# Layer-0 experts of a two-layer ViT tower: tokens sorted by expert through DRAM into 60 blocks

## The chip, the cores and the metric

The kernel runs on one core of a Trainium2 chip. A core has a matrix engine (TensorE, PE in the profile, with PEld for the loading of its weights), a vector engine (DVE), a scalar engine (ACT), a general one (POOL) and SyncE (SP), each with an instruction queue of its own that is worked off in order; SP, ACT and POOL can issue DMA transfers, which run on 16 shared DMA engines. The metric is the device time of the core in microseconds, the median of the runs of one kernel.

## The reference

Everything is float32. Four images of 3 x 224 x 224 become 784 patch tokens of 256 features each, which the tokenizer concatenates three times. Two layers follow: attention and a mixture of experts in each. The part that matters here is the mixture of layer 0, on 4 x 784 = 3136 distinct tokens:

```python
def _L0_ffn_ref(features, ...):                      # features: layer norm of h
    E, D, H, TOP_K = (6, 256, 256, 2)
    rh = jax.nn.relu(features @ router_w1 + router_b1)             # 128 wide
    expert_logits = jax.nn.softmax(rh @ router_w2 + router_b2, axis=-1)
    top_w, top_i = jax.lax.top_k(expert_logits, TOP_K)
    routing_weights = jax.nn.softmax(top_w, axis=-1)
    h1 = jax.nn.relu(jnp.einsum('bsd,edh->bseh', features, expert_w1) + expert_b1)
    h2 = jax.nn.relu(jnp.einsum('bseh,ehf->bsef', h1, expert_w2) + expert_b2)
    expert_out = jnp.einsum('bsef,efo->bseo', h2, expert_w3) + expert_b3
    sel = jnp.take_along_axis(expert_out, top_i[:, :, :, None], axis=2)
    return jnp.sum(sel * routing_weights[..., None], axis=2)
...
h = h + _L0_attn_ref(_layernorm(h, axis=-1), ...)
h = h + _L0_ffn_ref(_layernorm(h, axis=-1), ...)
h = h + _L1_attn_ref(_layernorm(h, axis=-1), ...)
h = h + _L1_ffn_ref(_layernorm(h, axis=-1), ...)
```

As written, all six experts run on every token, and two of the six results are kept.

## The kernel before

It carries one of the three copies of the tokens: 28 tiles of 112 tokens, 7 per image. The residual stream `h` stays in the on-chip memory, tokens on partitions: `h[TT, NT, D]` with TT = 112, NT = 28, D = 256. Stages follow each other: tokenizer, attention of layer 0, experts of layer 0, linear attention of layer 1, experts of layer 1, which also stores the result. A framework assigns buffers from pools, puts in the semaphore waits and orders the instructions of each engine's queue by priority; a pool that is closed gives its space to the next one opened, and the first use of that space waits for the last use of the old.

Products of a float32 operand take two records per instruction in the profile. A product reads its stationary operand into TensorE (PEld) and streams the columns of the other past it, into a bank of PSUM; there are seven such banks in the pool `psum` and one in `psum_s`. From there ACT or DVE must copy it out: `copy_out` (L71 on ACT, L73 on DVE) takes the two in turn, `bias_relu` (L78 on ACT, L80 on DVE) takes ACT two times in three. `transposed` (L227) turns tokens on partitions to features on partitions, by a product with an identity.

The experts of layer 0 (from the line `nxt = layer_input(work, 0, GT, "xT0")` on) go over 7 groups of 4 tiles (448 tokens). Per group: a router product (through `mm_t`, L236) with its relu (L504), the logits (L510), `top2` (L435 to L466: some 24 small vector instructions and two exponentials), which gives a weight for each of the six experts, 0 for those not chosen. Then the layer norm and the transposes of the next group, so that they lie between the experts' products. Then for each of the six experts two layers with features on partitions, two halves of 128 features each:

```python
pm = mm_t(GN, ew[e, i], slice(o * P, (o + 1) * P), lambda c: src[:, c, :], "pe")
bias_relu(dst[:, o, :], pm, col(b, 2 * e + o))
```

and the third with tokens on partitions (`mm_rows`, L247), whose result `add_weighted` (L487, DVE) multiplies with the expert's weight and adds to `h`. At the end of a group the weights are transposed (`weights_t`, L473, L475) and multiplied with the third bias (L537), which is added to `h` (L539). No transfer takes part in this stage but two weight loads for the next one (`Wqkv`, `Wout`) at its start. After it, the pool `lin` of layer 1's attention opens.

Of the kernel before, what the change touches and what calls it, by code (L numbers as in the profile page):

```python
"""ViT tower: patch tokenizer, one gated-attention + top-2 MoE layer, one linear-attention + top-2
gated-expert layer.

The tokenizer concatenates its tokens with themselves (q = k = tokens, so the sequence is three
copies of the 784 patch tokens).  Everything after it treats positions alike: rows are mapped
independently, and the two sums over the sequence (the attention logits of layer 0, the key norm and
key-value product of layer 1) are three times the sum over one copy, whatever the inputs.  The kernel
therefore carries one copy, puts the factor REP into those sums, and stores the rows three times.

Token tiles have 112 rows (7 per image).  The residual stream h stays in SBUF, tokens on partitions;  # L10
operands of the matrix products are transposed on the tensor engine to features on partitions.
"""
# [15 lines left out]
TT = 112  # tokens in a tile  # L28
NI = 4  # images
TPI = 7  # tiles in an image  # L30
# [10 lines left out]
GT = 4  # tiles in a group  # L41
# [3 lines left out]
E1 = 4  # L45
HEADS = 8
# [4 lines left out]
def tile_vit_tower(ctx: ExitStack, tc: tile.TileContext, a: dict, out: bass.AP):  # L51
# [15 lines left out]
    def copy_out(dst, src):  # L67
        """PSUM to SBUF, on the scalar and the vector engine in turn."""
        turn[0] += 1
        if turn[0] % 2:  # L70
            nc.scalar.copy(dst, src)  # L71
        else:
            nc.vector.tensor_copy(dst, src)  # L73
# [22 lines left out]
    rank = {}  # E, E-1, ..., 1 along the experts: the lower index wins a tie  # L96
# [5 lines left out]
    # Vectors that lie along partitions: rows of one tile, transposed once.  # L102
# [36 lines left out]
    def spread(pool, key, src):  # L139
        """A vector along the free dim, on all the partitions of a token tile."""  # L140
        n = src.shape[0]
        t = pool.tile([TT, n], F32, tag=key, name=key)
        nc.gpsimd.dma_start(out=t, in_=src.partition_broadcast(TT))
        return t

    def weight(pool, key, src, p=P, eng=nc.sync):
        """[K, N] as [p, K / p, N]."""
        k, n = src.shape
        t = pool.tile([p, k // p, n], F32, tag=key, name=key)
        eng.dma_start(out=t, in_=src.rearrange("(c p) n -> p c n", p=p))  # L150
        return t

# [1 line left out]
    # Partition (image, patch row); a strided view of the free dims is one patch column's patches.  # L154
# [28 lines left out]
    ew = {}  # L183
    for e in range(E0):
        for i, name in enumerate(("expert_w1", "expert_w2", "expert_w3")):
            ew[e, i] = weight(wts, f"ew{e}_{i}", a[f"L0_ffn_{name}"][e])
    eb3 = wts.tile([E0, D], F32, tag="eb3", name="eb3")
    nc.gpsimd.dma_start(out=eb3, in_=a["L0_ffn_expert_b3"])

    h = res.tile([TT, NT, D], F32, tag="h", name="h")  # L190

# [1 line left out]
    def ln_stats(src, n, twice=False):  # L193
        """Mean and 1 / sqrt(var + eps) of n tiles of rows.  twice: of a second layer norm, without
        an affine part between, as well: its input has mean 0 and variance var / (var + eps)."""
# [26 lines left out]
    def transposed(xn, n, put):  # L222
        """put(c, psum): the features c * 128... of n token tiles, on partitions."""
# [8 lines left out]
    def mm_t(n, w, wcols, xT, name, chunks=2):  # L232
        """(x @ w[:, wcols])^T, with the n columns of xT(c)."""
# [8 lines left out]
    def mm_rows(tiles, xT, w, name, chunks=2):  # L242
        """x @ w of up to two token tiles, in one PSUM bank: [TT, len(tiles), 256]."""
# [20 lines left out]
    with tc.tile_pool(name="tokw", bufs=2) as work:  # L264
        # Patches, features on partitions, tokens in the order of the sequence.
        pT = tokp.tile([KP, 2, NI * HP, HP], F32, tag="pT", name="pT")
        for w0 in range(0, HP, GT):
# [4 lines left out]
            for j in range(GT):  # L272
                # The reference has a patch's features in the order (y, x, channel).
# [57 lines left out]
    # Logits are dot products of whole images, per head: with (head, channel) on partitions,  # L331
    # products summed along the tokens, and then over a head's channels by a 0/1 matrix that leaves
    # the sum on each of them.
    scale = REP / math.sqrt(CHEAD) / math.sqrt(REP * SEQ)
    with tc.tile_pool(name="att", bufs=1) as attp:
# [3 lines left out]
        for tiles in groups:  # L339
# [3 lines left out]
            # The output bias goes into the residual now that the layer norm has read it.  # L343
# [77 lines left out]
    def top2(lg, n, E):  # L421
        """Routing weights over all experts, 0 off the two largest softmax(lg): softmax of those
        two probabilities.  lg: [TT, n, E], overwritten.  One more column of ones comes behind."""
# [35 lines left out]
        sel = chosen[0]  # L459
        nc.vector.tensor_tensor(sel, sel, chosen[1], ALU.add)  # L460
# [6 lines left out]
        return w  # L467

    def weights_t(pool, w, n, E):
        """w's tiles transposed: experts on partitions."""  # L470
# [21 lines left out]
    w1p = ctx.enter_context(tc.tile_pool(name="w1p", bufs=1))  # L492
    with tc.tile_pool(name="ffn0", bufs=2) as work:
# [3 lines left out]
        bout = spread(w1p, "bout", a["L1_attn_b_out"])  # L497

        nxt = layer_input(work, 0, GT, "xT0")
        for tiles in groups:  # L500
            t0 = tiles[0]
            xT = nxt
            rT = work.tile([P, GN], F32, tag="rT", name="rT")
            nc.scalar.activation(  # L504
                rT, mm_t(GN, rw1, slice(0, P), lambda c: xT[:, c, :], "pr"), AF.Relu,
                bias=col("router_b1"),
            )
            pr = psum_s.tile([P, 512], F32, tag="pss", name="plg")
            for j in range(GT):
                nc.tensor.matmul(  # L510
                    pr[:TT, j * E0 : (j + 1) * E0], rT[:, cut(j, 1)], rw2, start=True, stop=True
                )
            lg = small.tile([TT, GT, E0], F32, tag="lg0", name="lg0")
            nc.vector.tensor_tensor(
                lg, pr[:TT, : GT * E0].rearrange("p (j e) -> p j e", e=E0), over(rb2, GT), ALU.add
            )
            w = top2(lg, GT, E0)
            if t0 + GT < NT:
                nxt = layer_input(work, t0 + GT, GT, "xT0")
            for e in range(E0):  # L520
                src = xT
                for i, b in ((0, "eb1_0"), (1, "eb2_0")):
                    dst = work.tile([P, 2, GN], F32, tag=f"hid{i}", name=f"hid{i}")
                    for o in range(2):
                        pm = mm_t(
                            GN, ew[e, i], slice(o * P, (o + 1) * P), lambda c: src[:, c, :], "pe"
                        )
                        bias_relu(dst[:, o, :], pm, col(b, 2 * e + o))
                    src = dst
                for two in halves(range(GT)):  # L530
                    pm = mm_rows(two, lambda c, j: src[:, c, cut(j, 1)], ew[e, 2], "pe3")
                    add_weighted(pm, two, t0, w, e)
            wT = weights_t(work, w, GT, E0)
            for two in halves(range(GT)):
# [240 lines left out]
```

## Time and profile before

| | us |
|---|---|
| runs (3) | 1384.4, 1386.09, 1386.1 |
| median | 1386.09 |
| span of the profiled execution | 1382.7 |
| TensorE busy (its matmuls) | 1184.0 (86%) |
| TensorE, loading of weights | 719.4 (52%) |
| VectorE busy | 648.3 (47%) |
| ScalarE busy | 314.6 (23%) |
| POOL busy | 49.0 (4%) |
| granted TensorE clock, mean | 0.905 |

The profile is that of one execution. A line of a group of instructions tells the source line, engine, operation, what it writes and reads with the shapes, how often, then busy microseconds, mean nanoseconds of one, and the idle time of the engine just before them with what ended it. A line of the timeline tells start and length in microseconds, then the same, with the idle time before it in brackets. The clock that the throttle grants TensorE is given as a share of full speed, in tenths in the 40 slices of the span. Of the DMA issues, the last number is the microseconds from issue to landing; for some issues the profile has none.

### The profile page before, as it was taken

What the parts mean: (1) busy time and instruction counts of PE and PEld (TensorE: products, weight loads), DVE (VectorE), ACT (ScalarE), POOL (GpSimd) and SP (SyncE); (2) the same over time, 40 slices, a digit from 0 to 9 for tenths busy, and PEclk for the clock granted to TensorE, in tenths of its full rate; (3) what the DMA queues carried; (4) which work ended last, traced back from release to release, by engine and by line L of the source; (5) the groups of instructions that cost most, each with busy time, mean ns of one, the idle gap of its engine ahead of it and who ended that gap; (6) DMA issues with size and microseconds to landing.
All of it is one profiled execution on the core that took longest, in us unless ns stands there. A gap on an engine that the chain in (4) does not pass through costs nothing.

```text
span 1382.7 us, 11487 instructions
## 1 busy us (share of the span) xinstructions
PE 1184.0 (86%) x4073; PEld 719.4 (52%) x4073; DVE 648.3 (47%) x2008; ACT 314.6 (23%) x630; POOL 49.0 (4%) x54
## 2 busy tenths in 40 slices
PE   1576676798679999999999999979797889999997
PEld 0254554445455555555555555546565565555553
DVE  3844435948994342424343433443433435454353
ACT  0022122213333121212131212141423323111111
POOL 3000000210000000000000000100000000000000
PEclk9988777899889989999999999989797979997898
DMA  9000000000001000000000000100000000111112
GB/s 258 25 0 0 0 1 0 0 0 1 0 1 44 0 1 0 0 1 0 0 1 0 0 1 0 40 4 0 1 1 0 1 0 1 40 41 40 40 51 70
DMA packets 23153, 23.12 MB, mean 17 GB/s; under 512 B 3790, under 2 KB 22280, under 8 KB 23096
## 3 DMA queue, kind: packets, MB, share of 16 engines
q1 hardware_dynamic: 21820, 20.23, 5.0%
q10 hardware_dynamic: 252, 1.20, 0.4%
q0 software_dynamic: 1024, 0.96, 0.3%
q8 instruction: 32, 0.52, 0.2%
q14 instruction: 25, 0.20, 0.0%
HBM read 12.75 MB, written 9.63 MB: 16 GB/s over the span
## 4 chain that ended last, share of the span: by engine, by line
PE 76%; DVE 13%; ACT 7%; issue 2%; DMA 1%; ACTq 0%; SPq 0%; DVEq 0%
PE pe L236 21%; PE pe L247 11%; PE pwp L247 6%; PE pqk L578 4%; PE pt L227 4%; PE pe L724 3%; PE ps L236 3%; PE pkv L236 2%; PE pkv L644 2%; ACT qk L605 2%; DVE st L199 2%; PE pw L247 2%; PE pwo L247 2%; PE pe L713 2%; PE pwout L247 2%
## 5 line engine op out<-in xcount | busy, mean ns | idle before, releaser
L487 DVE SCALAR_TENSOR_TENSOR h<-pe,w,h 112x256 f32<-112x256 f32 x280 | 119.7, 478 | 150.9 <-PE pe L247 141.0
L247 PE MATMUL pe<-ew,hid 128*112 128x256 f32 x672 | 158.5, 385 | 1.8 <-ACT hid L78 1.4
L247 PEld LDWEIGHTS pe<-ew,hid 128*112 128x112 f32 x672 | 115.5, 177 | 53.2 <-ACT hid L78 17.3
L236 PE MATMUL pe<-hid,ew 128*128 128x448 f32 x336 | 140.3, 548 | 2.3 <-ACT hid L78 1.8
L78 ACT ACTIVATE hid<-pe,cols 128x448 f32<-128x448 f32 x112 | 70.9, 633 | 297.0 <-PE pe L236 296.2
L236 PE MATMUL pe<-xT,ew 128*128 128x448 f32 x336 | 135.3, 545 | 0.0
L236 PEld LDWEIGHTS pe<-hid,ew 128*128 128x128 f32 x336 | 61.5, 190 | 74.2 <-issue 41.8
L80 DVE TENSOR_SCALAR hid<-pe,cols 128x448 f32<-128x448 f32 x56 | 38.2, 683 | 128.6 <-PE pe L236 128.6
L227 PE MATMUL pt<-ident,xn 112*128 112x112 f32 x336 | 58.9, 313 | 41.5 <-DVE xn L217 41.5
L236 PEld LDWEIGHTS pe<-xT,ew 128*128 128x128 f32 x336 | 64.1, 193 | 49.3 <-issue 46.9
L227 PEld LDWEIGHTS pt<-ident,xn 112*128 112x128 f32 x336 | 45.4, 170 | 62.6 <-issue 56.9
L202 ACT ACTIVATE rstd<-mv,eps 112x4 f32<-112x4 f32 (+1 forms) x50 | 14.7, 297 | 202.2 <-DVE mv L200 202.0
L578 PE MATMUL pqk<-Wqkv,lxT 128*112 128x512 f32 x112 | 54.8, 644 | 1.0 <-ACT lxT L71 1.0
L638 PE MATMUL pn<-ones,uk 112*128 112x1 f32 x112 | 26.7, 342 | 33.5 <-ACT uk L618 33.5
L247 PE MATMUL pwo<-Wo,oT 128*112 128x256 f32 x112 | 32.7, 454 | 25.3 <-DVE oT L415 19.4
L247 PE MATMUL pwp<-Wp,sT 128*112 128x256 f32 x112 | 43.4, 572 | 11.7 <-ACT sT L319 11.7
L724 PE MATMUL pe<-eW,e 64*112 64x256 f32 x224 | 44.1, 408 | 3.3 <-ACT e L78 2.5
L236 PE MATMUL pe<-xT,eW 128*128 128x448 f32 x112 | 45.8, 546 | 0.0
L638 PEld LDWEIGHTS pn<-ones,uk 112*128 112x128 f32 x112 | 24.3, 303 | 38.5 <-ACT uk L618 38.5
L199 DVE BATCH_NORM_STATS2 st<-h 112x6 f32<-112x256 f32 x112 | 42.6, 410 | 0.7
L247 PEld LDWEIGHTS pwp<-Wp,sT 128*112 128x112 f32 x112 | 30.6, 280 | 23.1 <-ACT sT L319 13.2
L217 DVE TENSOR_SCALAR xn<-h,mv,rstd 112x256 f32<-112x256 f32 x112 | 42.4, 422 | 0.1
(194 smaller groups left out, 1631.4 us busy)
## 6 DMA issues: line engine op xcount, KB each, us to landing
out_dram<-h SPq DMA_DIRECT2D x84, 112.0 KB
ew<-in_L_ffn_expert_w_dram SPq DMA_DIRECT2D x18, 256.0 KB
img<-in_x_dram ACTq DMA_DIRECT2D x6, 196.0 KB
img<-in_x_dram SPq DMA_DIRECT2D x6, 196.0 KB
Wqkv<-in_L_attn_W_qkv_dram SPq DMA_DIRECT2D x1, 768.0 KB
eW<-in_L_ffn_eW_dram SPq DMA_DIRECT2D x5, 128.0 KB
Wp<-in_L_tok_Wp_dram SPq DMA_DIRECT2D x2, 256.0 KB
bqkv<-in_L_attn_b_qkv_dram POOLq DMA_DIRECT2D x1, 336.0 KB, 5.3
```

The lines of the kernel that those rows point to most:

```text
L78: nc.scalar.activation(dst, src, AF.Relu, bias=bias)
L80: nc.vector.tensor_scalar(dst, src, bias, 0.0, ALU.add, ALU.max)
L199: nc.vector.bn_stats(st[:, j, :], src(j))
L217: nc.vector.tensor_scalar(xn[:, j, :], src(j), mv[:, j, 0:1], r[:, j : j + 1], ALU.subtract, ALU.mult)
L227: nc.tensor.transpose(pt[:, j * TT : (j + 1) * TT], xn[:, j, c * P : (c + 1) * P], ident[:TT, :TT])
L236: nc.tensor.matmul(pm[: wcols.stop - wcols.start, :n], w[:, c, wcols], xT(c), start=(c == 0), stop=(c == chunks - 1),)
L247: nc.tensor.matmul(pm[:, i, :], xT(c, t), w[:, c, :], start=(c == 0), stop=(c == chunks - 1))
L487: nc.vector.scalar_tensor_tensor(ht, pm[:, i, :], w[:, j, e : e + 1], ht, ALU.mult, ALU.add)
L578: nc.tensor.matmul(pqk, xT[:, c, cut(j0 + j, 1)], Wqkv[:, c, : 2 * D], start=(c == 0), stop=(c == 1),)
L605: nc.scalar.activation(qk[:, j, i, :], qk[:, j, i, :], AF.Square, bias=mean[:, j, i : i + 1], accum_out=ss[:, j, i : i + 1],)
L638: nc.tensor.matmul(pn[:, c : c + 1], uk2[:, j, c * P : (c + 1) * P], ones[:TT], start=(j == 0), stop=(j == TPI - 1),)
L724: nc.tensor.matmul(pm[:, k, :], e2[rows_i, cut(j, 1)], eW3[rows_i, r, :], start=True, stop=True,)
```

## The change

The six experts no longer run on every token. The 28 tiles are taken in two halves of 14 (images 0 and 1, images 2 and 3), and in each:

- `routed` normalises and routes the tiles as before, in groups of 4, 3, 4, 3, keeps the normalised rows (`xr`), the two choices as 0/1 masks (`sel`) and their weights (`wk`), and adds the weighted third biases to `h`.
- `placed` gives each (token, choice) a row number in a table sorted by expert: counts before it in its tile (a product with a strictly triangular matrix), counts in the tiles before (a product with ones, and a running sum), and the expert's first row, with each expert's rows rounded up to blocks of 128. 30 blocks always suffice (`NB`). It also works out each block's expert (`ofi`) and its two biases (`bias`).
- `sent` writes each tile's rows, once for each choice, to their row numbers in a DRAM table `slots_x` by indirect DMAs on POOL's queue: 28 per half.
- `experts` goes over the 30 blocks: load 128 rows, then three layers, each of which transposes its input (two transposes), evicts that, with bias and relu for the second and third, and multiplies with the block's expert's weights, two products of 256 columns. All weights lie in one tile `ew`, which the product addresses by a register that TensorE loads, four blocks at a time. Tokens are on partitions after each product. The last result is stored to a DRAM table `slots_y`.
- `fetched` reads each tile's rows back, one indirect DMA for each choice, and adds them to `h` with their weights: 28 per half, with four buffers `yg`.

Routing, placing and sending of both halves stand ahead of the blocks of both. In the built program each engine's queue holds this: TensorE has half 0's routing, half 1's, then the 60 blocks strictly one after the other, only then layer 1. Every scatter waits for the one before it into the same table. On POOL, half 1's mask copies stand among half 0's first 17 scatters, its first scatter behind 21 of them; from there the two alternate until half 0's are out. On DVE, all routing and placing of both halves stand ahead of the first block's evictions, and half 0's 28 weighted adds stand among the evictions of half 1's first four blocks. On SP, block loads are issued up to six blocks ahead of the store they stand by. The first instructions of layer 1's attention on ACT, DVE and TensorE that touch its new pool wait for the last gather. The tables `slots_x` are filled with zeros once, by two DMAs behind the weights on SP's queue.

```diff
+SB = 128
+HT = NT // 2
+NB = (2 * HT * TT + E0 * (SB - 1)) // SB
+NTHR = -(-HT * TT // SB)
...
+    before = const.tile([TT, TT], F32, tag="before", name="before")
...
+    slots_x = [dram.tile([NB * SB, D], F32, tag=f"slots_x{i}", name=f"slots_x{i}") for i in range(2)]
+    slots_y = [dram.tile([NB * SB, D], F32, tag=f"slots_y{i}", name=f"slots_y{i}") for i in range(2)]
...
-    ew = {}
+    ew = wts.tile([P, E0, 3, 2, D], F32, tag="ew", name="ew")
...
+    blank = tokp.tile([SB, D], F32, tag="blank", name="blank")
+    nc.gpsimd.memset(blank, 0.0)
+    for x in slots_x:
+        nc.sync.dma_start(
+            out=x.rearrange("(i p) d -> p i d", p=SB),
+            in_=blank.unsqueeze(1).to_broadcast([SB, NB, D]),
+        )
...
-        return w
+        return w, first, chosen[1]
...
-        nxt = layer_input(work, 0, GT, "xT0")
-        for tiles in groups:
...
-            for e in range(E0):
-                src = xT
-                for i, b in ((0, "eb1_0"), (1, "eb2_0")):
-                    dst = work.tile([P, 2, GN], F32, tag=f"hid{i}", name=f"hid{i}")
-                    for o in range(2):
-                        pm = mm_t(
-                            GN, ew[e, i], slice(o * P, (o + 1) * P), lambda c: src[:, c, :], "pe"
-                        )
-                        bias_relu(dst[:, o, :], pm, col(b, 2 * e + o))
-                    src = dst
-                for two in halves(range(GT)):
-                    pm = mm_rows(two, lambda c, j: src[:, c, cut(j, 1)], ew[e, 2], "pe3")
-                    add_weighted(pm, two, t0, w, e)
...
+        def routed(half):
...
+                    w, *chosen = top2(lg, n, E0)
+                    for k in range(2):
+                        nc.gpsimd.tensor_copy(sel[:, k, j0 : j0 + n, :], chosen[k])
+                        mine = small.tile([TT, GT, E0], F32, tag="mine", name="mine")[:, :n]
+                        nc.vector.tensor_tensor(mine, w[:, :, :E0], chosen[k], ALU.mult)
+                        nc.vector.tensor_reduce(wk[:, j0 : j0 + n, k], mine, AX.X, ALU.add)
...
+        def placed(half, sel):
...
+            nc.tensor.matmul(pc[:TT, :ne], before, tk, start=True, stop=True)
+            nc.tensor.matmul(pc[:, ne : 2 * ne], allones, tk, start=True, stop=True)
...
+            slot = route.tile([TT, HT, 2], I32, tag="slot", name="slot")
+            nc.vector.tensor_copy(slot, at)
...
+        def sent(half, xr, slot):
+            for j in range(HT):
+                for k in range(2):
+                    nc.gpsimd.indirect_dma_start(
+                        out=slots_x[half][:, :],
+                        out_offset=bass.IndirectOffsetOnAxis(ap=slot[:, j, k : k + 1], axis=0),
+                        in_=xr[:, j, :], in_offset=None,
+                    )
+
+        def experts(half, ofi, bias):
+            for b0 in range(0, NB, 4):
+                n = min(4, NB - b0)
+                _, es = nc.values_load_multi_w_load_instructions(
+                    ofi[0:1, b0 : b0 + n], engines=[mybir.EngineType.PE], min_val=0,
+                    max_val=E0 - 1,
...
+                )
+                for b, e in zip(range(b0, b0 + n), es):
+                    xg = work.tile([SB, D], F32, tag="xg", name="xg", bufs=4)
+                    nc.sync.dma_start(out=xg, in_=slots_x[half][b * SB : (b + 1) * SB, :])
+                    act = xg
+                    for i in range(3):
+                        pt = ps_tile("pgt")
+                        for c in range(2):
+                            nc.tensor.transpose(
+                                pt[:, c * P : (c + 1) * P], act[:, c * P : (c + 1) * P], ident
+                            )
+                        aT = work.tile([P, 2, SB], F32, tag=f"aT{i}", name=f"aT{i}", bufs=3)
+                        if i == 0:
+                            copy_out(aT.rearrange("p c s -> p (c s)"), pt[:, :D])
+                        else:
+                            for c in range(2):
+                                bias_relu(
+                                    aT[:, c, :], pt[:, c * P : (c + 1) * P],
+                                    bias[:, i - 1, c, b : b + 1],
+                                )
+                        pm = ps_tile("pe")[:, :D]
+                        for c in range(2):
+                            nc.tensor.matmul(
+                                pm, aT[:, c, :], ew[:, bass.ds(e, 1), i, c, :],
+                                start=(c == 0), stop=(c == 1),
+                            )
+                        act = work.tile([SB, D], F32, tag=f"act{i}", name=f"act{i}", bufs=3)
+                        copy_out(act, pm)
+                    nc.sync.dma_start(out=slots_y[half][b * SB : (b + 1) * SB, :], in_=act)
+
+        def fetched(half, slot, wk):
+            for j in range(HT):
+                for k in range(2):
+                    yg = work.tile([TT, D], F32, tag="yg", name="yg", bufs=4)
+                    nc.gpsimd.indirect_dma_start(
+                        out=yg, out_offset=None, in_=slots_y[half][:, :],
+                        in_offset=bass.IndirectOffsetOnAxis(ap=slot[:, j, k : k + 1], axis=0),
+                    )
+                    ht = h[:, half * HT + j, :]
+                    nc.vector.scalar_tensor_tensor(
+                        ht, yg, wk[:, j, k : k + 1], ht, ALU.mult, ALU.add
+                    )
+
+        plan2 = []
+        for half in range(2):
+            xr, sel, wk = routed(half)
+            slot, ofi, bias = placed(half, sel)
+            sent(half, xr, slot)
+            plan2.append((slot, ofi, bias, wk))
+        for half in range(2):
+            slot, ofi, bias, wk = plan2[half]
+            experts(half, ofi, bias)
+            fetched(half, slot, wk)
```

## The prediction

> **What bounds the kernel now.** I read the slices first: TensorE is busy in nine tenths or more of nearly every slice from the 13th to the 25th, at nearly the full clock. Then a table of windows, to cut out the stage that the change rewrites: it runs from 416.7 us (the copy after the attention's last product) to 892.9 us (the first copy of layer 1), 476 us, with TensorE busy for 464 of them at a granted clock of 0.98. Last the timeline of one expert on one group of four tiles.
>
> ```profile
> PE   1576676798679999999999999979797889999997
> PEclk9988777899889989999999999989797979997898
> ```
> The windows' columns are start and end, length, busy time and count of TensorE, of its weight loads, of VectorE, ScalarE and POOL, the granted clock, the DMA share and GB/s:
> ```profile
> 416.70:892.90 476.20, 463.59 (x1568) 272.69 (x1568) 176.02 (x494) 100.98 (x162) 5.29 (x5) 0.98 0.01 4
> 160.00:164.00 4.00, 3.54 (x8) 2.62 (x9) 0.00 (x0) 2.30 (x3) 0.00 (x0) 0.50 0.00 0
> 168.00:172.00 4.00, 2.50 (x12) 1.74 (x10) 3.09 (x9) 0.00 (x0) 0.00 (x0) 1.00 0.00 0
> ```
> ```profile
> 441.47 3.17 PE L236 MATMUL pe<-xT,ew 128*128 128x448 f32 x8
> 444.48 3.17 PE L236 MATMUL pe<-hid,ew 128*128 128x448 f32 x8
> 447.68 3.71 PE L247 MATMUL pe<-ew,hid 128*112 128x256 f32 x16
> ...
> 428.10 1.12 PE L247 MATMUL pe<-ew,hid 128*112 128x256 f32 x4 [1.38 <-ACT hid L78]
> 160.46 2.05 PE L247 MATMUL pwp<-Wp,sT 128*112 128x256 f32 x4 [2.06 <-ACT sT L319]
> 418.19 0.36 PE L227 MATMUL pt<-ident,xn 112*128 112x112 f32 x2
> 912.71 0.61 PE L227 MATMUL pt<-ident,q 112*128 112x112 f32 x2 [0.56 <-DVE q L629]
> ```
>
> The three starts 441.47, 444.48 and 447.68 and the next one at 451.22 give 9.75 us for an expert on a group, without a gap: each product streams while the eviction of the one before is under way. 42 of them (7 groups, 6 experts) are 410 us of the stage. The 66 left over are routing and start. So TensorE's stream is the bound, and the change removes two thirds of the expert products. What it puts there does not stream: the last four lines are what the same instructions cost after a wait, at full clock (1.12 for four, 0.36 for two) and at half (2.05 and 0.61; the windows at 160 and 168 us show both clocks).
>
> **The change, step by step, on the path.** The new stage is a chain: route half 0, place, scatter it, 60 blocks, fetch half 1. All is counted against 476 us.
>
> *Blocks.* TensorE gets its instructions block by block, so nothing of the next block fills a block's waits but its first two transposes. A block is three times: two transposes, eviction, two products of 256 columns (four records), eviction. An eviction starts some 0.04 after the product ends and the next product 0.05 after the eviction (the copy at 416.75 follows a product ending at 416.71). The evictions, from
>
> ```profile
> L71 ACT COPY lxT<-pt 128x448 f32<-128x448 f32 x4 | 2.1, 532 | 26.1 <-PE pt L227 26.1
> L71 ACT COPY lxT<-pt 128x336 f32<-128x336 f32 x4 | 1.8, 438 | 10.4 <-PE pt L227 10.4
> L73 DVE COPY lxT<-pt 128x448 f32<-128x448 f32 x4 | 2.4, 611 | 0.1
> L73 DVE COPY lxT<-pt 128x336 f32<-128x336 f32 x4 | 2.0, 498 | 0.0
> L78 ACT ACTIVATE hid<-pe,cols 128x448 f32<-128x448 f32 x112 | 70.9, 633 | 297.0 <-PE pe L236 296.2
> ```
>
> by their slopes: 256 columns take 0.37 on ACT and 0.41 on DVE, and 128 columns of an activation 0.37 (633 less 320 columns at 0.83 ns). Five of a block's six stand on the path, with their starts 0.41 + 0.45 + 0.40 + 0.41 + 0.40 = 2.07; of each pair of biased halves only the first, as the product of the other half comes later. At full clock TensorE adds 3 x 1.17 + 2 x 0.41 + 0.2 (the first transposes follow the last product) = 4.53, at half 3 x 2.10 + 2 x 0.66 + 0.4 = 8.0. A block is 6.6 or 10.1 us, 60 blocks 396 or 606. Which clock? In a half-clock block TensorE streams some 6.5 of 10.1 us (twice the 3.3 worked out for the third rival). The window at 160 us is busy for 3.54 of 4 and still at half; the one at 168 keeps full clock at 2.50 of 4. A loop that comes out of a wait therefore starts at half and leaves it only in a dense stretch; its densest 3 us or so (last products, then transposes) are about three quarters streamed. I take half the clock for 7 blocks in 10: 9.05 each, 543 us.
>
> The Trainium skill ("TensorE: Matmul & The Clock Gate", Part 1) gives full clock after some 3.4 us of sustained work and half only after an idle window of that length; by the idle rule alone no window in a block is idle, the loop would soon be and stay at full clock, and the sum would be 147 us lower. The rows above show half clock beside much busy time, so the sum leans to them.
>
> *Scatters.* POOL issues 28 per half, and each waits until the one before into the same buffer has landed, as they may overlap in DRAM. One therefore costs a whole landing:
>
> ```profile
> gb<-in_L_ffn_gb_dram POOLq DMA_DIRECT2D x1, 1.8 KB, 3.1
> bout<-in_L_attn_b_out_dram POOLq DMA_DIRECT2D x1, 112.0 KB, 5.9
> ```
>
> from 3.1 (112 rows of 16 bytes, alone in its queue) to 5.9 (112 rows of 1 KB behind a larger load). No row shows addresses taken from a tile. I take 4.0, nearer to the quiet row since the DMA share of this stage is 0.01 and each now runs alone: 28 x 4.0 = 112 us (87 to 165). Half 1's routing and placing (68) lie beneath them: its mask copies stand in POOL's queue behind the first 17 scatters of half 0, its own first scatter behind 21, and 7 of half 0 alternate with half 1's. The other 20 of half 1 lie under half 0's blocks.
> The skill ("DMA: Bandwidth & Descriptors", Anatomy of one DMA) gives 2.0 us and the bytes at 436 GB/s for a DMA from this queue, 2.3 for 112 KB, which would make 64 us of the 112; the trace's shortest landing is 3.1, so that is not used.
>
> *Routing* loses its cover: before, it ran between experts' products. In the trace a group's first product is at 417.3 and its weights are ready at 428.9; transposing the weights to the last add takes 480.9 to 485.8. With ends that overlap 15.5 a group, 4 groups of half 0: 62 us (54 to 66). The four extra vector instructions and two POOL copies a group hide in it. *Placing* to the slot numbers: two small products, a copy and some 16 vector instructions of 0.2 to 0.3 us: 6 (5 to 8).
>
> *Register loads*, 16, one per four blocks, on TensorE. No row shows one. Least 0, beneath the first eviction; most a landing of 3.1 less 0.4, 43 in all. I take 8, as the value is long in SBUF.
>
> *Fetches.* A gather that reads its 112 rows: 0.53 (POOL's time for a direct issue) to 3.1 (one at a time). Four buffers allow four in flight, 4.0 / 4 = 1.0; I take 1.1. After the last block: its store (3), 27 x 1.1, the last landing (4) and add: 37 (21 to 95). Layer 1's tiles take the space of this stage, so its first copies wait for the last gather; nothing covers it. Half 0's 28 adds stand in DVE's queue among half 1's first four blocks, and the evictions behind them wait: 28 x 1.1 + 5 against 4 x 9 leaves little, I take 10 (0 to 30). First block load: 3.
>
> *At nothing:* the zero fill (7.9 MB, behind the weights on SP's queue) has until 484 us, covered by tokenizer and attention; uncovered it is some 30 us at the 258 GB/s of the first slice. Block loads run four blocks ahead. The constants on POOL and DVE stand ahead of small loads, 1 us at most. The 168 weighted adds that go (L487, 478 ns) were off the path.
>
> Sum: 62 + 6 + 112 + 3 + 543 + 8 + 10 + 37 = 781 against 476: +305. The profiled execution's span is 1382.7; the runs shown (median 1386.09) lie 3.4 above, so 1386.1 + 305 = 1691 us.
>
> **The rivals.**
> - *Full clock in the loop.* For it: 168 us keeps its clock at low load. Against: the loop begins cold. 396 for 543: 1544.
> - *Half clock throughout and slow scatters.* Landings of 5.9 as beside other traffic, 606 for the blocks: 1691 + 53 + 63 = 1807. Against: the queue is quiet.
> - *Not slower: blocks overlap on TensorE.* Seven PSUM buffers and three of each operand would let block b + 1 stream through the evictions of b. Streaming alone is 12 x 0.22 + 6 x 0.10 = 3.3 a block, 197 in all, stage 435, time 1345. The point where it decides: the other pieces are 238, so 60 blocks would need 238 or less, 4.0 each. Against: the block order of TensorE's instructions.
>
> **How the numbers follow.** The forecast 0.55 (1610 to 1775 by clock, scatter and gather), full clock 0.25, half clock and slow scatters 0.18, not slower 0.02. Range: the forecast's with full clock's 1544 and part of the slowest, 1530 to 1810. What this kernel's measurement can tell from no change is 0.2%; slower 0.98, within 0.01, faster 0.01.
>
> **What would show it.** In the new profile: blocks of 6.6 to 10 us with TensorE busy half to two thirds of them and a clock well under 0.98 in the loop; a stretch of about 110 us with TensorE nearly idle and POOL issuing one DMA per landing; some 35 us idle ahead of layer 1. Wrong if scatters follow each other faster than they land, if blocks overlap, if register loads cost microseconds each, or if DVE stalls tens of us at half 1's start.

## The result, and the profile after

| | before | after |
|---|---|---|
| median of the runs | 1385.58 us (4 runs, 1384.4 to 1386.1) | 1733.2 us (4 runs, 1732.2 to 1734.05) |
| ratio to before | 1 | 1.2507, 95% interval 1.249 to 1.2525 |
| span of the profiled execution | 1382.7 us | 1731.9 us |
| mean granted clock | 0.905 (0.98 in the stage) | 0.711 |

The change costs 349 us of span. The slices of the page, each 43.3 us long, show where: the expert stage now runs from the 10th into the 29th.

```profile
PE   1576678875664467777767777773487887999998
PEclk9887779988555695555555555555688988998977
```

TensorE is at seven tenths with a five under it: half the clock, over some 600 us, with one short island (the 6 and the 9). Cut by windows, with start and end, length, busy time and count of TensorE, its weight loads, VectorE, ScalarE and POOL, then clock, DMA share and GB/s:

```profile
416.70:490.30 73.60, 41.43 (x132) 24.63 (x132) 43.68 (x208) 16.18 (x29) 2.94 (x10) 0.61 0.07 21
490.30:579.10 88.80, 35.39 (x106) 21.64 (x105) 33.71 (x155) 4.88 (x14) 35.73 (x45) 0.51 0.16 50
579.10:869.90 290.80, 214.74 (x547) 122.89 (x548) 39.93 (x101) 49.87 (x141) 18.24 (x21) 0.60 0.12 37
869.90:924.00 54.10, 35.81 (x81) 19.92 (x81) 25.39 (x81) 10.31 (x28) 30.52 (x30) 0.50 0.27 79
924.00:1188.90 264.90, 202.48 (x456) 115.34 (x456) 33.15 (x84) 41.08 (x116) 0.00 (x0) 0.50 0.07 23
1188.90:1232.20 43.30, 1.46 (x8) 1.11 (x6) 21.94 (x55) 0.59 (x2) 28.14 (x29) 0.50 0.26 77
1232.20:1731.90 499.70, 447.06 (x1576) 269.90 (x1576) 209.89 (x709) 116.21 (x317) 11.77 (x8) 0.86 0.08 23
```

In order: half 0's routing and placing (73.6), half 0's scatters (88.8), the 60 blocks (three windows, 609.8, the middle one with half 0's fetch among them), half 1's fetch (43.3), layer 1 (499.7, where it was 489.8 before). The stage begins at 416.7 us as before, so the zero fill costs nothing ahead of it.

A block, in TensorE's timeline (start, duration, line and operation, count, and in brackets the idle time ahead of it with what ended it). A block begins with the transposes of xg; the first four lines are a block at full clock, the last three one at half:

```profile
639.18 0.38 PE L697 MATMUL pgt<-ident,xg 128*128 128x128 f32 x2
640.08 1.13 PE L711 MATMUL pe<-ew,aT 128*128 x4 [0.52 <-ACT aT L75]
641.73 0.44 PE L697 MATMUL pgt<-ident,act 128*128 128x128 f32 x2 [0.52 <-DVE act L77]
...
646.11 0.38 PE L697 MATMUL pgt<-ident,xg 128*128 128x128 f32 x2
...
665.65 0.63 PE L697 MATMUL pgt<-ident,xg 128*128 128x128 f32 x2
666.80 2.07 PE L711 MATMUL pe<-ew,aT 128*128 x4 [0.52 <-ACT aT L75]
...
676.06 0.64 PE L697 MATMUL pgt<-ident,xg 128*128 128x128 f32 x2
```

From 639.18 to 646.11 is 6.93 us, from 665.65 to 676.06 is 10.41. The blocks at full clock have 6.8 to 7.1 and those at half, but for a few, 10.41 to 10.62 (10.53 on the average). Only 7 run wholly at full clock, between 597 and 646 us, and the two beside them partly. Each idle of 0.44 to 0.52 in front of a product or transpose is an exposed eviction. Nothing of another block fills it. TensorE waits for a block load only at the first block. A block with a register load ahead of its first product is no longer than its neighbours.

### The profile page after: what moved, and what is told of

The parts are those of the page before. It is cut to its first block, busy times and chain, and to the rows that moved or that the text cites. A ratio compares the mean times of both kernels' runs of the same rounds, so it can differ in the third digit from the quotient of the medians.

```text
span 1731.9 us, 12362 instructions
## 1 busy us (share of the span) xinstructions
PE 1259.6 (73%) x3821; PEld 755.6 (44%) x3821; DVE 663.1 (38%) x2161; ACT 329.3 (19%) x791; POOL 158.1 (9%) x187
## 4 chain that ended last, share of the span: by engine, by line
PE 66%; DVE 15%; ACT 10%; issue 5%; DMA 3%; POOL 1%; another core or an unknown queue 0%; ACTq 0%; SPq 0%; DVEq 0%; POOLq 0%
PE pe L711 20%; PE pgt L697 6%; PE pwp L288 5%; PE pt L268 3%; PE pqk L780 3%; PE pe L926 3%; PE pe L277 3%; PE ps L277 2%; PE pkv L277 2%; ACT aT L82 2%; PE pkv L846 2%; DVE st L240 2%; ACT qk L807 2%; PE pw L288 2%; PE pb L591 2%
## 5 line engine op out<-in xcount | busy, mean ns | idle before, releaser
L711 PE MATMUL pe<-ew,aT 128*128 x720 | 350.6, 637 | 91.1 <-ACT aT L82 40.9
L711 PEld LDWEIGHTS pe<-ew,aT 128*128 128x128 f32 x720 | 198.4, 305 | 189.4 <-ACT aT L82 71.4
L77 DVE COPY act<-pe 128x256 f32<-128x256 f32 x120 | 51.0, 425 | 363.6 <-PE pe L711 359.3
L697 PE MATMUL pgt<-ident,act 128*128 128x128 f32 x240 | 78.4, 427 | 65.7 <-ACT act L75 32.2
L82 ACT ACTIVATE aT<-pgt,bias 128x128 f32<-128x128 f32 x160 | 54.3, 365 | 261.2 <-PE pgt L697 161.2
L697 PEld LDWEIGHTS pgt<-ident,act 128*128 128x128 f32 x240 | 33.2, 195 | 146.6 <-ACT act L75 72.1
L780 PE MATMUL pqk<-Wqkv,lxT 128*112 128x512 f32 x112 | 55.3, 649 | 43.3 <-issue 42.6
L723 POOL DMA_INDIRECT yg<-slots_y,slot x56 | 52.1, 930 | 255.9 <-DMA slots_y<-act 234.6
L676 POOL DMA_INDIRECT slots_x<-xr,slot x56 | 52.2, 933 | 91.5 <-DMA slots_x<-xr,slot 77.0
L697 PE MATMUL pgt<-ident,xg 128*128 128x128 f32 x120 | 36.3, 402 | 27.2 <-DMA xg<-slots_x 27.2
L529 DVE SCALAR_TENSOR_TENSOR h<-pe,w,h 112x256 f32<-112x256 f32 x112 | 46.4, 476 | 12.0 <-PE pe L926 12.0
```

The source lines that it names most:

```text
L82: nc.scalar.activation(dst, src, AF.Relu, bias=bias)
L529: nc.vector.scalar_tensor_tensor(ht, pm[:, i, :], w[:, j, e : e + 1], ht, ALU.mult, ALU.add)
L676: nc.gpsimd.indirect_dma_start(out=slots_x[half][:, :], out_offset=bass.IndirectOffsetOnAxis(ap=slot[:, j, k : k + 1], axis=0), in_=xr[:, ...
L697: nc.tensor.transpose(pt[:, c * P : (c + 1) * P], act[:, c * P : (c + 1) * P], ident)
L711: nc.tensor.matmul(pm, aT[:, c, :], ew[:, bass.ds(e, 1), i, c, :], start=(c == 0), stop=(c == 1),)
L723: nc.gpsimd.indirect_dma_start(out=yg, out_offset=None, in_=slots_y[half][:, :], in_offset=bass.IndirectOffsetOnAxis(ap=slot[:, j, k : k + ...
```

## The experiments

The changed kernel is the base of all runs, and the time to compare with is 1733.2 us unless said. The prediction left three things unsettled: why the loop is at half clock, whether the scatters' stretch is a sum of landings, and what a block would cost if blocks overlapped. The result added a fourth: 10 us in layer 1, which the change does not touch.

### More work per block, to test the clock

```
-                        for c in range(2):
+                        for c in (0, 1, 0, 1) if i == 0 else (0, 1):
                             nc.tensor.transpose(
```

> Each block's two input transposes are done twice (same data into the same place), so TensorE has more to do per block and the path is longer by two transposes of 128 columns: about 0.2 us at full clock, 0.4 at half. The result is unchanged. Theory (the loop sits at half clock because its densest stretches fall just short of what brings the full clock back; the product of the last layer and the next block's transposes are the densest place): the added work lifts exactly that stretch, most blocks run at 7.2 us in place of 10.5, and the kernel, though it does more, gets faster: 1733 less 100 to 195, that is 1540 to 1635 us, granted clock in the loop above 0.8. Rival (the clock is low for a reason that TensorE's load in the loop does not touch): half clock stays, blocks of 10.9 to 11.0, 1755 to 1763 us.

And the same for all three layers:

```
-                        for c in range(2):
+                        for c in (0, 1, 0, 1):
```

> All six transposes of a block are done twice. Path longer by 0.65 us a block at full clock, 1.3 at half. The result is unchanged. Theory of the clock (more load in the loop, more full clock): nearly all blocks at full clock, 7.6 to 7.8 us each, 460 to 480 for the 610 of the loop: 1585 to 1610 us. If one dense stretch a block is enough (the run with only the input transposes doubled is already at full clock), this one is slower than that by some 26 us. Rival (clock not touched by load): 11.8 a block, 1805 to 1815 us.

Measured: 1650.8 us (1643 to 1654) and 1608.8 us (1608 to 1623). The kernel that does more is faster, by 82 and by 124 us. The windows over the two loops, of the first run and then of the second:

```profile
577.70:1107.60 529.90, 370.09 (x1202) 222.10 (x1203) 102.39 (x266) 101.35 (x285) 48.65 (x50) 0.76 0.13 40
```
```profile
576.90:1064.10 487.20, 325.17 (x1442) 207.04 (x1443) 102.79 (x266) 101.43 (x285) 48.76 (x50) 0.95 0.14 43
```

Some 120 and 360 more matmul records, and the clock goes from 0.55 (the mean over the three windows of the changed kernel's loop) to 0.76 and 0.95. So the clock does follow TensorE's load in the loop, and the rival falls. The first run missed its range by 16 us, and its clock the 0.8 expected, since it goes up and down: blocks of 7.0 to 7.8 us stand between blocks of 8 to 11. One dense stretch a block brings the full clock back, but does not hold it. The second run is inside its range (1585 to 1610) with blocks of 7.5 to 8.0 us nearly throughout. That it would be some 26 us slower than the first was said for the case that the first is already at full clock, which it is not.

The windows of the changed kernel in stretches of 3.4 us, laid so that the clock changes at their edges, show how narrow it was (columns as above):

```profile
588.40:591.80 3.40, 2.94 (x9) 1.98 (x8) 0.42 (x1) 0.37 (x1) 0.93 (x1) 0.50 0.26 76
591.80:595.20 3.40, 2.13 (x9) 1.04 (x7) 0.42 (x1) 0.88 (x3) 0.93 (x1) 1.00 0.31 102
...
646.40:649.80 3.40, 1.85 (x8) 1.07 (x8) 0.96 (x3) 0.74 (x2) 0.00 (x0) 1.00 0.23 77
649.80:653.20 3.40, 2.38 (x6) 1.09 (x5) 0.14 (x2) 0.74 (x2) 0.00 (x0) 0.51 0.00 0
653.30:656.70 3.40, 2.88 (x7) 2.02 (x8) 0.67 (x2) 0.37 (x1) 0.00 (x0) 0.50 0.00 0
```

A half-clock stretch busy for 2.94 us is followed by the full clock, one busy for 2.88 us is not. At full clock a stretch busy for 1.85 us is followed by half, while TensorE worked in every block. These are single stretches of one execution, and their length and place were chosen to fit the changes; where exactly the bounds lie stays open.

The Trainium skill ("TensorE: Matmul & The Clock Gate", Part 1) has the clock fall after an idle window of about 3.4 us. The stretch at 646.4 was not idle, and the clock fell after it; here the measurement decides.

### Blocks side by side

Two blocks, and then four, pass through the three layers together (g is 2 or 4; the edit is abridged, and the block's tiles also get more buffers, `xg` 8 for 4, `aT` and `act` 4 for 3):

```
+                for p0 in range(0, n, g):
+                    blk = list(range(p0, min(p0 + g, n)))
...
+                    for i in range(3):
+                        for q in blk:
+                            (two transposes of block q, eviction)
+                        for q in blk:
+                            (two products of block q, eviction)
```

> Two blocks go through the three layers side by side, so TensorE has the other block's products while one is evicted; the number of instructions is the same. Theory (a block is a chain of latencies, five exposed evictions of 0.5 us, and the low clock comes from the gaps): a pair takes 8.4 to 9.2 us at full clock, 4.2 to 4.6 a block, 252 to 276 us for 60 in place of 610: 1375 to 1400 us. If the clock stays at half: 6.6 a block, about 1520. Rival (ScalarE and VectorE, the register-addressed weights or the block loads bound a block): blocks stay near 7 us and above even at full clock, 1540 or more.

> Four blocks side by side. Theory (latency chain): TensorE streams without gaps at full clock; streaming alone is 3.3 us a block, so 3.3 to 3.8 a block, 200 to 230 us in place of 610: 1320 to 1355 us, under the kernel before. Rival (evictions bound: six a block on two engines, about 2.2 us of ScalarE and VectorE together, with starts): no better than pairs, 1375 to 1400 us.

Measured: 1396.9 us (ratio to before 1.0081, 1.0065 to 1.0098) and 1354.0 us (0.9779, 0.9763 to 0.9796), both inside the ranges of the theory. TensorE's timeline with four at a time:

```profile
621.21 1.04 PE L702 MATMUL pgt<-ident,xg 128*128 128x128 f32 x8
622.11 3.72 PE L717 MATMUL pe<-ew,aT 128*128 x16
625.67 1.12 PE L702 MATMUL pgt<-ident,act 128*128 128x128 f32 x8
626.62 3.67 PE L717 MATMUL pe<-ew,aT 128*128 x16
...
634.58 1.04 PE L702 MATMUL pgt<-ident,xg 128*128 128x128 f32 x8
```

No brackets: TensorE waits for nothing. From 621.21 to 634.58 are 13.37 us for four blocks, 3.34 each, which is the prediction's streaming alone of 3.3. The loop takes 232 us where it took 610, at a clock of 0.95; at 3.34 a block it would be 200, and most of the rest lies at half 1's start, where half 0's fetch runs and three groups of four take 65.0 us in place of 40.1. With the same number of instructions this shows that a block was its chain of exposed evictions, at a clock that these gaps brought down; neither the evictions as work (ScalarE is busy for 91 and VectorE for 97 of the 232 us) nor the block loads nor the register-addressed weights bound it. The added buffers are no rival: in the changed kernel's loop TensorE waited for evictions, not for free buffers or loads.

### The scatters

> The copies of the chosen masks (16, two a group of tiles) go from POOL to ScalarE; nothing else changes. Theory: half 1's eight mask copies stand in POOL's queue between half 0's scatters, and the five places where a scatter of half 0 began later than 2.8 us after the one before lost 8 to 10 us in all; without the copies half 0's 28 scatters follow each other at 2.8 us and the first block starts 6 to 10 us earlier: 1723 to 1727 us. Rival (the copies filled time in which POOL waited for landings anyway): 1732 to 1734.

```
-                        nc.gpsimd.tensor_copy(sel[:, k, j0 : j0 + n, :], chosen[k])
+                        nc.scalar.copy(sel[:, k, j0 : j0 + n, :], chosen[k])
```

Measured 1760.2 us, 27 longer, and both theories miss. First, the stretch from the first scatter to the first block is 88.6 us, as before (88.8). POOL's timeline shows why:

```profile
542.76 0.93 POOL L676 DMA_INDIRECT slots_x<-xr,slot  x1 [1.86 <-DMA slots_x<-xr,slot]
545.56 0.93 POOL L676 DMA_INDIRECT slots_x<-xr,slot  x1 [1.87 <-DMA slots_x<-xr,slot]
554.27 0.93 POOL L676 DMA_INDIRECT slots_x<-xr,slot  x1 [7.78 <-DVE mine L667]
555.50 0.93 POOL L676 DMA_INDIRECT slots_x<-xr,slot  x1 [0.30 <-issue]
```

Half 0's scatters follow each other at 2.80 us, with three gaps of 3.0 to 3.3, up to the 21st at 545.56. The one at 554.27 is half 1's first, which stands there in the queue and waits 7.78 us for half 1's routing and placing (its slot numbers, L646, are written at 553.82, beside the L667 that the profile names). Half 0's last seven come behind it. In the changed kernel the mask copies, which wait for half 1's routing too, held the scatters back by about as much (the 21st is at 554.13), so that half 1's first had only 1.30 us left to wait, at 556.36; without them POOL reaches the same wait earlier. Second, the loop has 635 us at a clock of 0.50: in this run only one stretch, at 590 us, got the full clock, and the 26 us that the island had saved are gone. The blocks are the same. Layer 1 has 505 us in this run, 6 more than in the others: TensorE is busy for 452.7 us of it in place of 447.1, with the same 1576 records and a clock of 0.85 for 0.86. Why the clock is lower there stays unexplained.

> First and second choice of a token are scattered into two buffers in DRAM, each zeroed; a block loads its 128 rows from both and VectorE adds them. The result is unchanged: a slot is filled in one of the two. Scatters into the two buffers need not wait for each other, so a chain is 14 long. Theory (a scatter costs its whole landing, 2.8 us, because it waits for the one before into the same buffer): two scatters per 2.8 us, half 0's stretch falls from 87 us to some 45; VectorE is not done with half 1's routing then, and the first block's eviction stands behind most of it, so the first blocks gain 25 to 35 us of the 42: 1698 to 1708 us. Rival (POOL or the DMA queue sets the pace, not the wait): 1733 or more, with the added 60 loads and adds.

```
-                        out=slots_x[half][:, :],
+                        out=slots_x[2 * half + k][:, :],
...
+                        nc.sync.dma_start(out=x2, in_=slots_x[2 * half + 1][b * SB : (b + 1) * SB, :])
+                        nc.vector.tensor_tensor(xg, xg, x2, ALU.add)
```

Measured 1732.4 us, the time of the rival, yet POOL's timeline and the windows (the scatters, then the loop) show the theory's mechanism:

```profile
502.94 0.93 POOL L676 DMA_INDIRECT slots_x<-xr,slot  x1 [0.30 <-DMA slots_x<-xr,slot]
504.51 0.93 POOL L676 DMA_INDIRECT slots_x<-xr,slot  x1 [0.63 <-DMA slots_x<-xr,slot]
505.74 0.93 POOL L676 DMA_INDIRECT slots_x<-xr,slot  x1 [0.30 <-DMA slots_x<-xr,slot]
```
```profile
488.60:550.90 62.30, 35.21 (x107) 21.67 (x108) 29.00 (x131) 4.89 (x14) 27.97 (x36) 0.52 0.26 77
550.90:1187.50 636.60, 482.68 (x1083) 273.53 (x1083) 124.65 (x350) 101.63 (x285) 56.87 (x58) 0.50 0.15 45
```

Two scatters now go out every 2.80 us, so it is the wait, not POOL, that sets the pace. The first block starts 28 us earlier (its transposes come right behind half 1's count products on TensorE, not behind an eviction on VectorE as expected), and the loop, at half clock from end to end, is 27 us longer. The total alone would have said that the scatters don't matter. With the clock no longer in the way, on the kernel with four blocks side by side (1354.0 us), the queue was tested again: the mask copies on ScalarE, and half 1's scatters behind half 0's (the edit in short).

```
+                        if half == 0 and b == 0:
+                            later = xg[:TT, :28] * 0.0 + slot of half 1
+                            sent(1, xr of half 1, later)
```

> The kernel with four blocks side by side (1354 us), with the mask copies on ScalarE and half 1's scatters held back until half 0's first block load has landed (their slot numbers are taken from a copy that also reads that load, times zero). So nothing of half 1 stands between half 0's scatters on POOL's queue. Theory (in the changed kernel, and in the run with the mask copies moved alone, half 0's last seven scatters waited behind half 1's first, which waited for half 1's routing): 28 scatters at 2.79 us from 489, the first block's transposes at 569 to 570 in place of 577.8, the kernel 1345 to 1348 us. Rival (half 0's scatters had no time to lose there, since the first blocks wait for VectorE in any case, or half 1's scatters now disturb the first block loads): 1353 to 1358.

Measured 1341.1 us (ratio to before 0.9679, 0.9663 to 0.9695), 4 under its range. From the first scatter to the first block:

```profile
490.90:572.40 81.50, 35.34 (x106) 21.59 (x105) 33.67 (x155) 6.55 (x22) 26.07 (x28) 0.52 0.14 43
```

81.5 for 88.8: 28 scatters at 2.8 us and the first load. The loop too is shorter here, 225 for 232 us, which was not expected; the gain lies at half 1's start, where the three groups of four blocks take 57.3 us in place of 65.0. Why stays open.

### The fetch at the end

> Half 1's fetch is issued after layer 1's first image (of half 0), and the tiles it needs get a pool of their own, so that layer 1's do not wait for them (layer 1's attention output has one buffer in place of two to make the space). Theory (the 43 us between the last block's product and layer 1's first copy are the fetch, and nothing else has to wait for it): layer 1 starts about 3 us after the last block, the 28 gathers run under image 0, their 13 us of adds mostly in VectorE's gaps: 1690 to 1702 us. Rival (VectorE or POOL is as full in layer 1, and the wait comes back at image 1): 1715 to 1733.

```
-            fetched(half, slot, wk)
+            if half == 0:
+                fetched(half, slot, wk)
...
         for b in range(NI):
+            if b == 1:
+                fetched(1, slot, wk)
```

Measured 1702.3 us, 31 less, at the slow end of the theory's range. The stretch between the last product and layer 1's first copy falls from 43.3 to 2.6 us; layer 1 takes 511.6 for 499.7. Of the 41 us won, 12 come back there. Whether it is the 28 adds or the attention output's single buffer that costs these 12 was not tried.

### Layer 1

> The counter by which evictions are dealt to ScalarE and VectorE in turn is set, ahead of layer 1, to the 210 that it has there in the kernel before; the change leaves it at 524, which is 2 further in the turn of three that the biased evictions use. Nothing else changes. Theory: layer 1, which took 489.8 us before and 498.9 to 500.9 in the changed kernel and all variants of it so far, is longer for this alone: 1722 to 1725 us. Rival (layer 1 is longer because the granted clock or the DMA traffic is different when it starts): 1732 to 1734.

```
+    turn[0] = 210
     with tc.tile_pool(name="lin", bufs=2) as lin:
```

Measured 1725.0 us, 8 less; the window of layer 1 in this run:

```profile
1231.70:1722.20 490.50, 439.27 (x1576) 266.39 (x1576) 209.50 (x709) 115.98 (x317) 11.78 (x8) 0.87 0.08 23
```

490.5, against 499.7 in the changed kernel and 489.8 before. The counter that deals evictions to ScalarE and VectorE is shared by the whole kernel. The new blocks leave it two steps further in its turn of three, and with that alone layer 1 is 9 us longer. Of these, 7.8 are TensorE's busy time for the same 1576 records (447.1 against 439.3, at a clock of 0.86 against 0.87); by what path the dealing moves the clock is not shown. It fits the 499 to 501 us that layer 1 had in the runs above, whatever the stage in front of it took, but for the 505 of one and the 511.6 with the fetch in it.

### All together

Four blocks side by side, mask copies on ScalarE, two scatter buffers, the late fetch and the counter.

> Four blocks side by side, the mask copies on ScalarE, two scatter buffers, half 1's fetch after layer 1's first image, and the dealing counter set to 210 ahead of layer 1, all together. By stage, from the runs made singly: first scatter at 489 us as in the others; half 0's two chains land by 531 (28 at 1.4 us), VectorE is done with half 1's routing at about 555, so the first quad is slow; the loop's 232 us then end at 775 to 785; layer 1 starts 3 us later and takes 490 plus the 12 us that the late fetch costs it. 1385.6 is the kernel before. Theory (the parts add, since with four blocks side by side the clock no longer hangs on chance): 1272 to 1295 us. Rival (VectorE, with the added adds, bounds the loop): 1310 or more.

Measured 1295.8 us (ratio to before 0.9363, 0.9339 to 0.9388), 0.8 above the range. The loop has 234 us at a clock of 0.97, layer 1 begins 2.5 us after it and takes 503.7. The first block starts at 551 rather than 531: its transposes stand in TensorE's own queue behind half 1's routing products, the last of which starts at 550.84. This version beats both kernels: the sorting does remove two thirds of the expert products, and pays if the blocks stream.

## Why the prediction was right, and where its terms were off

The forecast of 1691 us was 42 short of 1733.2. Direction, mechanism and order of the terms were as predicted; the sizes were not, and that the total came so near is partly luck, since a scatter stretch taken 26 us too long covers part of blocks taken 60 us too short:

| term of the sum | predicted | measured | why |
|---|---|---|---|
| routing half 0 | 62 | 66.8 | up to the count products at 483.5 us |
| placing | 6 | 6.9 | |
| scatters and first load | 115 | 88.8 | each 2.8, not 4.0; but held by some 7 us for half 1's routing |
| blocks | 543 | 602.8 | 10.53 and 7.0 for 10.1 and 6.6, and 51 of 60 at half clock for 42 |
| register loads | 8 | 0 | no block is longer for one |
| stall at half 1's start | 10 | 6.9 | five blocks take 59.5, not 52.7; cause in part open |
| tail fetch | 37 | 43.3 | 1.23 a gather for 1.1, and a 2.3 us addition on POOL ahead of it |
| layer 1 | 0 | +9.9 | the dealing counter |

*Blocks.* The step that failed by most is the number of blocks at half clock: 7 in 10 were taken, 51 of 60 came. At the measured sizes 7 in 10 would give 568 us; so the sizes make 25 us of the miss and the share the other 35. The sizes were off by 0.4 a block at either clock: the five waits were booked at 0.46 (0.41 and the 0.05 ahead of the next product) and are 0.50 on the average, and the second and third pair of transposes, taken at 0.36 and 0.61 from rows of 112 columns, have 128 and take 0.44 and 0.69; the products add the rest. The reasoning from windows (a loop that comes out of a wait leaves the half clock only in a dense stretch) was right, and the two runs with doubled transposes show it. That the share could be read to a tenth was not: the stretches above differ by 0.06 us of busy time, and two edits that left TensorE's instructions as they were (the mask copies on ScalarE, and the two buffers, which add a load and a VectorE addition a block) left no block wholly at full clock.

*Scatters.* The price of one was taken between bounds from 3.1 to 5.9 us, and the measured spacing of 2.80 lies under both. It goes to the quiet row, as the text argued, and past it. The estimate from the Trainium skill's figure ("DMA: Bandwidth & Descriptors", Anatomy of one DMA), 2.3 us, which the prediction set aside, was nearer than the 4.0 taken. The prediction named the places of half 1's mask copies and of its first scatter in POOL's queue and gave them no cost. In the changed kernel the copies hold half 0's scatters by some 8 us (the 21st at 554.13, where 2.8 each from 490.32 would give 546.3) and half 1's first scatter by another 0.7. At 2.8 us each without these waits the stretch is 81.5. Nor was TensorE nearly idle in it, as the signs of the prediction had it: half 1's routing keeps it busy for 35.4 of the 88.8 us.

*Stall.* The size was near (6.9 for 10). In TensorE's timeline of the changed kernel it is one block; two lines of VectorE and ScalarE stand below it:

```profile
888.28 2.07 PE L711 MATMUL pe<-ew,aT 128*128 x4 [0.52 <-issue]
892.74 0.69 PE L697 MATMUL pgt<-ident,act 128*128 128x128 f32 x2 [2.39 <-issue]
894.81 2.08 PE L711 MATMUL pe<-ew,aT 128*128 x4 [1.38 <-DVE aT L84]
901.23 0.69 PE L697 MATMUL pgt<-ident,act 128*128 128x128 f32 x2 [4.34 <-ACT act L75]
```
```profile
892.26 0.42 DVE L77 COPY act<-pe 128x256 f32<-128x256 f32 x1 [2.17 <-remote]
900.81 0.37 ACT L75 COPY act<-pe 128x256 f32<-128x256 f32 x1 [5.59 <-remote]
```

The predicted mechanism, half 0's adds ahead of VectorE's evictions, does not explain these lines: ahead of both copies the engine sat idle, and the profile cannot name what released it ("remote"). What held them stays open. In the run with the dealing counter set, whose instructions are the same up to layer 1, the mechanism is there to see: adds that wait for their gathers stand ahead of the copy for which TensorE then waits 3.53 us.

```profile
906.35 0.48 DVE L728 SCALAR_TENSOR_TENSOR h<-yg,wk,h 112x256 f32<-112x256 f32 x1 [1.36 <-DMA yg<-slots_y,slot]
907.57 0.48 DVE L728 SCALAR_TENSOR_TENSOR h<-yg,wk,h 112x256 f32<-112x256 f32 x1 [0.73 <-DMA yg<-slots_y,slot]
908.44 0.69 PE L697 MATMUL pgt<-ident,act 128*128 128x128 f32 x2 [3.53 <-DVE act L77]
```

*Tail.* Predicted as uncovered because layer 1's tiles take this stage's space; the 42.63 us in front of layer 1's first product and the run with the late fetch confirm it:

```profile
1188.66 1.70 PE L268 MATMUL pt<-ident,xn 112*128 112x112 f32 x8
1232.99 3.75 PE L780 MATMUL pqk<-Wqkv,lxT 128*112 128x512 f32 x4 [42.63 <-issue]
```

*The rivals.* Full clock in the loop (1544) did not come by itself; the kernel with all transposes doubled, at 0.95, came to 1609. Half clock throughout with slow scatters (1807) was half right: nearly half clock throughout, fast scatters. Blocks that overlap on TensorE did not come with the change, but four side by side took 1354, where 1345 was worked out. The price of a streaming block (3.3) was right; that the totals agree is partly luck, as the loop took 35 us more than its 197 and the scatters 26 less than their 115.

## What to carry to other kernels

Where a matmul stage turns from a stream into a chain, price it twice: the waits that are now exposed, and the clock that these waits bring down; then look for independent chains to put side by side before anything else. In a queue that is served in order, look for the first instruction whose data come from another chain of work, and price everything behind it. And read an experiment by its stages: a total can hide a gain of 28 us behind a loss of 27 elsewhere.

## What was not expected of the hardware

Two more transposes a block made the kernel 82 us faster, and an edit outside the loop (the mask copies) changed the loop's time by 26 us through the clock. A scatter of 112 rows of 1 KB to addresses from a tile takes 2.8 us from one to the next when each waits for the last, 0.93 of it on POOL; gathers that do not wait follow each other at 1.23 us.
